# Attention, clustering and MLP on one core: the start of the first image, where two projections change their PSUM banks and one set of exponentials changes its place

## The chip, the cores and the metric

The kernel runs on one core of one Trainium2 chip. The metric is the device time of one execution in microseconds (us). The matmul engine is called PE here, the vector engine DVE, the scalar engine ACT, the GpSimd engine POOL, and SP is the engine that issues most of the transfers (DMAs).

## The reference, cut to what matters

Four images of 256 channels and 64 x 64 pixels (4096 positions) go through two layers. The change lies at the very start of the first layer, for the first image.

```python
def _L0_conv_ref(x, wq, bq, wk, bk, wv, bv, gamma):
    B, Cc, H, W = x.shape
    N = H * W                                   # 4096
    xf = x.reshape(B, Cc, N)
    q = jnp.einsum('oc,bcn->bno', wq, xf) + bq  # 32 channels
    k = jnp.einsum('oc,bcn->bon', wk, xf) + bk[None, :, None]
    attn = jax.nn.softmax(jnp.einsum('bnd,bdm->bnm', q, k), axis=-1)
    v = jnp.einsum('oc,bcn->bon', wv, xf) + bv[None, :, None]
    out = jnp.einsum('bcn,bmn->bcm', v, attn).reshape(B, Cc, H, W)
    return gamma[0] * out + x
```

The second layer (group norm, a 1x1 convolution into features and values, a clustering by the highest similarity, a projection, an MLP with a GELU, and two batch norms with ReLU) follows for each image. Only two of its details matter here: a small product of its weights, `wf`, is made at the start of the kernel, and its constants are worked out once on DVE (`derived`).

## The kernel before, in words

The order of all instructions is written out by hand (`tc.manual_schedule()`): each engine works through its own list in the order in which the program issues it, and waits by semaphores. Which buffer a tile gets is decided by the pools: a tile of a tag waits until the tile that had its buffer before has been read for the last time.

The attention of an image is cut into 64 units: 8 blocks of 512 queries by 8 groups of 512 keys. One unit `u` passes through these steps:

- `half(u, h)` for h = 0, 1 (line 420): PE makes two products of 128 keys by 512 queries into a tile `sc` of two PSUM banks; ACT copies it into `s` in SBUF (line 433); DVE takes the running maximum `top` (line 444).
- After the eight units of a block, the maximum is folded (line 501), turned over by PE (`turned_over`, line 506), reduced over keys and spread into a diagonal by DVE (`across`, lines 513 and 515), and broadcast by a matmul with ones into the tile `hold` (`spread`, line 573).
- `exps(u)`: DVE subtracts the maximum in two instructions (line 583), and ACT takes the exponentials in three (lines 588, 589, 592). The first writes into the second bank of `hold`.
- `factors(u)`: DVE forms `t31` (line 616, printed as tile `t`), and POOL forms further sums (line 595). They are the operands of a product by seven multiplications instead of eight.
- `weigh(u)`: PE multiplies them with the values into four banks `av` (line 679): first the term with `s` alone (`av<-s,v`), then the one with `t31` (`av<-t,v`).

For the first image the function `alone` brings the attention to the point where the loop over units begins. Its stages are: the values of the first half of the image; `staged("first")`, the projections of keys and queries of the first 2048 positions; more values; `staged("second")`, those of the other 2048 positions; then the eight units of block 0, with a pair of value tiles (`v_pair`) after each of the first six; then fold, turn-over, the first half of unit 8 (`half(GRP, 0)`, "the ninth score"), the last values, the broadcast, `wf`, the second half of unit 8, and `exps(0)` and `factors(0)`. After that `weighting` takes over: `exps(1)`, then `weigh(0)`, with the scores of later units between the parts.

A projection is stored "halved": ACT rounds it to a first half (line 335), DVE forms the rest (line 336), and SP writes four copies of these parts to DRAM for the keys and four for the queries (line 342). From there the units load their keys (`k_unit`, line 398) and queries (`q_block`, line 392). `staged` projects both keys and queries into one two-bank tile of the pool `ps_s` before it halves either; `halved` does it for one of them, in a one-bank tile of the pool `ps_m`, and its two parts go into a work buffer of the tag `t13`.

The pools in question have two buffers each:

```python
    ps_s = ctx.enter_context(tc.tile_pool(name="ps_s", bufs=2, space=PSUM))
    ps_m = ctx.enter_context(tc.tile_pool(name="ps_m", bufs=2, space=PSUM))
```

`ps_s` holds the scores `sc`, the tile of `staged`, and `hold` (which keeps one of its two buffers from the first broadcast on). `ps_m` holds the values `vp` (two halves to a tile, `v_half`, copied out by ACT at line 383), the turned-over maximum `tt`, the tile of `wf` (lines 256 and 259, copied out by ACT at lines 260 and 261), and two of the four banks `av`. `t31` lies in the tag `t13` too.

Of the kernel before, what the change touches and what calls it, by code (L numbers as in the profile page):

```python
# [29 lines left out]
RG, GRP = 4, N // NB  # L30
# [23 lines left out]
def attention_then_cluster_block(  # L54
# [197 lines left out]
    def wf():  # L252

        tps = ps_m.tile([P, NB], F32, tag="m", name="wf_p")
        for k in range(KC):
            nc.tensor.transpose(
                tps[:ED, k * P : (k + 1) * P], own_w["mix"][:, k, 0, 16 : 16 + ED], ident
            )
        nc.tensor.matmul(tps[:, C : C + ED], fb_w, ident[:ED, :ED], start=True, stop=True)
        nc.scalar.copy(wf_t, tps[:ED, :C])  # L260
        nc.scalar.copy(fvb[:, :ED], tps[:, C : C + ED])
# [43 lines left out]
    def attention(b, xs, ys):  # L305
# [7 lines left out]
        def projected(which, i, ps):  # L313

            col = 1 if which == "k" else 0
            for k in range(KC):
                for r in range(RG):
                    nc.tensor.matmul(
                        ps[r * D : (r + 1) * D],
                        wqk_s[:, k, col],  # L320
                        block(xs, k, 4 * i + r),
                        start=(k == 0),
                        stop=(k == KC - 1),
                    )

        def halves_of(which, i, hi, lo, ps, dma=nc.sync):

            col = 1 if which == "k" else 0
            if which not in own:
                own[which] = dram.tile([NBLK // RG, P, 4, NB], F32, tag=which, name=f"{which}_{b}")
            bias = bqk_s[:, col : col + 1]
            nc.scalar.activation(hi, ps, AF.Identity, bias=bias)
            nc.vector.scalar_tensor_tensor(
                lo, ps, bias, hi.bitcast(F32), ALU.add, ALU.subtract
            )
            rows = own[which][i]
            for c in range(4):  # L340
                part = hi if c in ((0, 2) if which == "k" else (0, 1)) else lo
                dma.dma_start(out=rows[:, c], in_=part.bitcast(F32))
# [6 lines left out]
        def staged(name, which, dma=nc.sync):  # L349


            st = spool.tile([P, 4, NB], F32R, tag="s", name=f"st_{b}_{name}")
            ps = ps_s.tile([P, 2, NB], F32, tag="s", name=f"pr_{b}_{name}")
            for j, (w, i) in enumerate(which):
                projected(w, i, ps[:, j])
            for j, (w, i) in enumerate(which):
                halves_of(w, i, st[:, 2 * j], st[:, 2 * j + 1], ps[:, j], dma)

        def halved(which, i):

            ps = ps_m.tile([P, NB], F32, tag="m", name=f"{which}p_{b}_{i}")
            two = work.tile([P, 2, NB], F32R, tag="t13", name=f"hl_{which}_{b}_{i}")
            projected(which, i, ps)
            halves_of(which, i, two[:, 0], two[:, 1], ps)
# [3 lines left out]
        def v_half(i):  # L368
            if i == 0:
                own["v"] = big.tile([P, N // P, C], F32, tag="v", name=f"v_{b}")  # L370
            if i % 2 == 0:
                vps[0] = ps_m.tile([P, 2, C], F32, tag="m", name=f"vp_{b}_{i // 2}")
            o = (i * P) % XT
            for k in range(KC):
                nc.tensor.matmul(  # L375
                    vps[0][:, i % 2, :],
                    xs[i * P // XT][:, k, o : o + P],
                    wv_s[:, k, :],
                    start=(k == 0),
                    stop=(k == KC - 1),  # L380
                )
            if i % 2:
                nc.scalar.copy(own["v"][:, i - 1 : i + 1, :], vps[0])

        def v_pair(i):
            v_half(2 * i)
            v_half(2 * i + 1)
# [12 lines left out]
        def begun(u):  # L400

            if u in slots:
                return
            nb, g = divmod(u, GRP)
            if u + 1 < units:
                k_unit(u + 1)

            pool, tag = {SLOTS: (swap, "w1"), SLOTS + 1: (swap, "w2")}.get(
                u % (SLOTS + 2), (spool, "s")
            )  # L410
            slots[u] = pool.tile([P, 4, 2, QW], F32, tag=tag, name=f"s_{b}_{u}")
            if g == 0:
                tops[nb] = work.tile([P, 2, NB], F32, tag="top", bufs=1, name=f"top_{b}_{nb}")
# [15 lines left out]
        def tiles(t):  # L429
            return t.rearrange("p r (h n) -> p r h n", h=2)  # L430

        def kept(u, h, sc):
            nc.scalar.copy(slots[u][:, PAIR[h]].rearrange("p h r n -> p r h n"), tiles(sc))  # L433
# [18 lines left out]
        def half(u, h, kept_only=False):  # L452

            nb, g = divmod(u, GRP)
            if h == 0:
                begun(u)
            sc = products(u, h)
            kept(u, h, sc)  # L460
            own_copy = slots[u][:, PAIR[h]].rearrange("p h r n -> p r h n")
            if g == 0 and h == 0:
                highest_of(nb, own_copy)
            elif g == 0 or kept_only:
                held.append(lambda: highest_of(nb, own_copy))
            else:
                return lambda: highest_of(nb, tiles(sc))
            return lambda: None
# [125 lines left out]
        def plus(out, x, y, op=ALU.add):  # L594
            nc.gpsimd.tensor_tensor(out, x, y, op)  # L595

        def factors(u):

            nb, g = divmod(u, GRP)
            s = slots[u]
            if g == 0:
                accs[nb] = work.tile([P, 2, 2, QW], F32, tag="acc", bufs=1, name=f"acc_{b}_{nb}")
            one, both = accs[nb][:, 0], accs[nb][:, 1]
            if g >= SEVEN:
                if g == SEVEN:
                    plus(both, both, one, ALU.subtract)
                for acc, q in ((both, B11), (one, B12), (both, B21), (one, B22)):
                    eng = nc.vector if acc is one and nb == NBLK - 1 else nc.gpsimd  # L610
                    eng.tensor_tensor(acc, acc, s[:, q], ALU.add)  # L611
                return
            b12 = own["hold"][:, 1].rearrange("p (r n) -> p r n", r=2).unsqueeze(1)
            t31[u] = work.tile([P, 2, 2, QW], F32, tag="t13", name=f"t13_{b}_{u}")
            t4s[u] = work.tile([P, 2, QW], F32, tag="t4", bufs=1, name=f"t4_{b}_{u}")
            nc.vector.tensor_tensor(  # L616
                t31[u], s[:, B11 : B22 + 1 : 2], b12.to_broadcast([P, 2, 2, QW]), ALU.add
            )
            plus(s[:, B12], t31[u][:, 1], s[:, B11])
            plus(t4s[u], s[:, B12], s[:, B21])  # L620
            if g == 0:
                plus(both, s[:, B12], s[:, B21])
            else:
                plus(one, t31[u - 1][:, 1] if g == 1 else one, t31[u][:, 1])
                plus(both, both, t4s[u])
# [183 lines left out]
        def alone():  # L809

            roots()
            for i in range(3):
                v_pair(i)
            staged("first", (("k", 0), ("q", 0)))
            k_unit(0)
            q_block(0)
            q_block(1)
            for i in range(3, 8):
                v_pair(i)
            for g in range(4):  # L820
                for f in sums(g):
                    f()
            for u in range(GRP):
                if u == 0:
                    begun(0)
                    staged("second", (("k", 1), ("q", 1)))
                    rest = load_rest()
                for h in range(2):
                    half(u, h)()
                caught(1)  # L830
                if u < 6:
                    v_pair(u + GRP)
                if u > 1:
                    next(rest, None)
            fold(0)
            for g in range(4, SEVEN):
                for f in sums(g):
                    f()
            tp = turned_over(0, ps_m.tile([P, 4, P], F32, tag="m", name=f"tt_{b}_0"))
            half(GRP, 0)  # L840
            v_pair(14)
            dgs["dg"] = across(0, "w2", tp)
            spread(0, dgs["dg"])
            v_pair(15)
            wf()
            half(GRP, 1)
            exps(0)
            factors(0)

        def maximum():  # L850
            dgs["dg"] = across(0, "t")
# [1187 lines left out]
```

## Time and profile before

| what | value |
|---|---|
| median of 3 runs | 3199.19 us (3198.45 to 3201.14) |
| the profiled execution, own time | 3196.98 us |
| its span, first to last instruction | 3195.0 us |
| PE busy | 3085.5 us, 97% of the span |
| DVE busy | 2537.0 us, 79% |
| POOL busy | 2260.6 us, 71% |
| ACT busy | 1734.8 us, 54% |
| mean granted PE clock | 0.990 |

Two microseconds of the profiled execution lie outside its span, and the execution is 2.2 us shorter than the median of the runs. Over the whole span PE is the engine with the least idle time; what a stage at the start is worth is read from its own waits, since all later work follows from it. The column PEclk of the tables by stretch is the share of full speed that the clock of PE was granted in that stretch; 0.50 means that matmuls ran at half speed.

### The profile page before, as it was taken

What the parts mean: (1) busy time and instruction counts of PE and PEld (TensorE: products, weight loads), DVE (VectorE), ACT (ScalarE), POOL (GpSimd) and SP (SyncE); (2) the same over time, 40 slices, a digit from 0 to 9 for tenths busy, and PEclk for the clock granted to TensorE, in tenths of its full rate; (3) what the DMA queues carried; (4) which work ended last, traced back from release to release, by engine and by line L of the source; (5) the groups of instructions that cost most, each with busy time, mean ns of one, the idle gap of its engine ahead of it and who ended that gap; (6) DMA issues with size and microseconds to landing.
All of it is one profiled execution on the core that took longest, in us unless ns stands there. A gap on an engine that the chain in (4) does not pass through costs nothing.

```text
span 3195.0 us, 40473 instructions
## 1 busy us (share of the span) xinstructions
PE 3085.5 (97%) x13890; PEld 2445.7 (77%) x13890; DVE 2537.0 (79%) x3649; ACT 1734.8 (54%) x2719; POOL 2260.6 (71%) x2127
## 2 busy tenths in 40 slices
PE   7999999999999999999999999999999999998999
PEld 5777887788677787768867788786876787875786
DVE  3888888677788888867778888877778888887675
ACT  4556654545556665445555666544556566654444
POOL 3888886378488888547848888855766888883663
PEclk8999999999999999999999999999999999999999
DMA  5122126100112123510011222431111112150000
GB/s 164 40 63 63 60 61 182 63 21 30 47 50 63 53 60 94 155 50 28 23 56 44 66 60 63 111 123 50 30 44 43 54 60 64 56 149 2 14 21 27
DMA packets 105868, 200.33 MB, mean 63 GB/s; under 512 B 14416, under 2 KB 30400, under 8 KB 104128
## 3 DMA queue, kind: packets, MB, share of 16 engines
q1 hardware_dynamic: 101856, 181.94, 17.9%
q0 software_dynamic: 2976, 14.70, 2.5%
q8 instruction: 110, 1.80, 0.2%
q10 hardware_dynamic: 832, 1.11, 0.1%
q14 instruction: 94, 0.77, 0.1%
HBM read 149.37 MB, written 48.34 MB: 62 GB/s over the span
## 4 chain that ended last, share of the span: by engine, by line
PE 42%; POOL 24%; DVE 19%; issue 8%; ACT 6%; DMA 1%; POOLq 0%; SPq 0%; ACTq 0%; DVEq 0%
PE mo L1651 10%; POOL acc L595 9%; PE av L679 6%; PE hq L1734 5%; DVE top L444 5%; DVE s L583 4%; POOL t L595 4%; POOL s L595 4%; DVE t L616 3%; PE hp L1734 3%; PE hr L1734 3%; PE fv L1225 3%; PE sc L420 3%; POOL acc L611 2%; PE vp L375 2%
## 5 line engine op out<-in xcount | busy, mean ns | idle before, releaser
L433 ACT COPY s<-sc 128x1024 f32<-128x1024 f32 x512 | 514.8, 1011 | 506.3 <-PE sc L420 500.1
L583 DVE TENSOR_TENSOR s<-s,hold 128x1024 f32<-128x1024 f32 x512 | 598.7, 1209 | 28.9 <-ACT hold L566 15.0
L595 POOL TENSOR_TENSOR s<-t,s 128x512 f32<-128x512 f32 x224 | 303.5, 1355 | 356.1 <-DVE t L616 287.6
L679 PE MATMUL av<-t,v 128*128 128x256 f32 x1792 | 464.8, 382 | 12.8 <-DVE t L616 11.7
L679 PE MATMUL av<-s,v 128*128 128x256 f32 x1792 | 460.8, 379 | 2.2 <-ACT s L589 2.2
L595 POOL TENSOR_TENSOR acc<-acc,t 128x512 f32<-128x512 f32 x352 | 461.2, 1329 | 0.0
L679 PE MATMUL av<-s,sum 128*128 128x256 f32 x1792 | 459.5, 379 | 0.0
L420 PE MATMUL sc<-q,k 128*128 128x512 f32 x1024 | 405.6, 480 | 36.8 <-DMA k<-k 10.5
L444 DVE TENSOR_TENSOR top<-sc,top 128x1024 f32<-128x1024 f32 x326 | 397.8, 1220 | 29.7 <-ACT s L433 24.8
L1689 ACT ACTIVATE hs<-hs,pv_s 128x256 f32<-128x256 f32 x496 | 232.3, 502 | 343.5 <-DVE hs L1725 343.5
L616 DVE TENSOR_TENSOR t<-s,hold 128x1024 f32<-128x1024 f32 x224 | 272.7, 1217 | 159.3 <-ACT s L592 71.0
L679 PEld LDWEIGHTS av<-t,v 128*128 128x128 f32 x1792 | 338.4, 190 | 70.1 <-DVE t L616 21.4
L1651 PE MATMUL mo<-hs,w 128*128 128x256 f32 x1512 | 385.3, 381 | 0.0
L679 PEld LDWEIGHTS av<-s,v 128*128 128x128 f32 x1792 | 340.3, 190 | 57.8 <-ACT s L589 2.6
L679 PEld LDWEIGHTS av<-s,sum 128*128 128x128 f32 x1792 | 339.4, 189 | 54.5 <-issue 1.9
L1651 PEld LDWEIGHTS mo<-hs,w 128*128 128x128 f32 x1512 | 283.0, 190 | 47.2 <-ACT hs L1689 6.4
L595 POOL TENSOR_TENSOR t<-s 128x512 f32<-128x512 f32 x224 | 295.7, 1320 | 17.6
L420 PEld LDWEIGHTS sc<-q,k 128*128 128x128 f32 x1024 | 176.6, 190 | 144.0 <-DVE top L444 70.2
L592 ACT ACTIVATE s<-s 128x1024 f32<-128x1024 f32 x256 | 267.5, 1045 | 1.2
L1725 DVE TENSOR_TENSOR hs<-hq,hs 128x256 f32<-128x256 f32 x496 | 198.8, 421 | 79.2 <-PE hq L1734 69.3
L588 ACT ACTIVATE hold<-s 128x512 f32<-128x512 f32 x224 | 135.1, 603 | 221.5 <-DVE s L583 221.4
L679 PE MATMUL av<-t,sum 128*128 128x256 f32 x896 | 231.7, 381 | 0.0
(299 smaller groups left out, 5349.1 us busy)
## 6 DMA issues: line engine op xcount, KB each, us to landing
k<-k SPq DMA_DIRECT2D x256, 256.0 KB, 2.7
x<-in_x SPq DMA_DIRECT2D x62, 512.0 KB, 6.6
out<-xn SPq DMA_DIRECT2D x62, 256.0 KB, 2.1
att<-t SPq DMA_DIRECT2D x56, 256.0 KB, 3.9
x<-att POOLq DMA_DIRECT2D x12, 1024.0 KB, 8.7
q<-q SPq DMA_DIRECT2D x32, 256.0 KB, 4.1
w<-in_w SPq DMA_DIRECT2D x8, 1024.0 KB, 10.3
rden<-row_rd SPq DMA_DIRECT2D x28, 256.0 KB, 3.7
```

Source lines behind the costliest of these rows:

```text
L420: nc.tensor.matmul(sc[:, r, :], k_s[:, (2 * h + r) * P : (2 * h + r + 1) * P], qs[u // GRP], start=True, stop=True,)
L433: nc.scalar.copy(slots[u][:, PAIR[h]].rearrange("p h r n -> p r h n"), tiles(sc))
L444: nc.vector.tensor_tensor(top, src, top if saved[nb] is None else saved[nb], ALU.max)
L583: nc.vector.tensor_tensor(sh, sh, mb.to_broadcast([P, 2, 2, QW]), ALU.subtract)
L592: nc.scalar.activation(s[:, PAIR[1]], s[:, PAIR[1]], AF.Exp)
L595: nc.gpsimd.tensor_tensor(out, x, y, op)
L616: nc.vector.tensor_tensor(t31[u], s[:, B11 : B22 + 1 : 2], b12.to_broadcast([P, 2, 2, QW]), ALU.add)
L679: nc.tensor.matmul(av[bank][:, half_ * QW : (half_ + 1) * QW], a[:, r], t[:, r], start=(g == 0 and r == 0 and i in (1, 7, 2, 4)), stop=(g ...
L1651: return nc.tensor.matmul(bank[:, half * HB : (half + 1) * HB], a[:, j], t, start=start, stop=stop)
L1689: nc.scalar.activation(src, src, AF.Gelu_apprx_tanh, bias=pvc("b1", P, j + 4 * (i > 1)))
L1725: nc.vector.tensor_tensor(dst, ps, term, ALU.add)
L1734: nc.tensor.matmul(out, w, x, start=True, stop=True)
```

## The change

In `alone`, the second projections go through `halved`, keys first, then queries, so they use two one-bank tiles of `ps_m` (the values' banks) in place of a two-bank tile of `ps_s`. After the turn-over, the pair of values 14 is split: one half is made ahead of the broadcast, the other after `exps(0)` and `factors(0)`. The pair 15, the second half of unit 8 and `wf` come after them too, and `wf` comes last.

```diff
             for u in range(GRP):
                 if u == 0:
                     begun(0)
-                    staged("second", (("k", 1), ("q", 1)))
+                    halved("k", 1)
+                    halved("q", 1)
                     rest = load_rest()
                 for h in range(2):
                     half(u, h)()
...
             tp = turned_over(0, ps_m.tile([P, 4, P], F32, tag="m", name=f"tt_{b}_0"))
             half(GRP, 0)
-            v_pair(14)
+            v_half(28)
             dgs["dg"] = across(0, "w2", tp)
             spread(0, dgs["dg"])
-            v_pair(15)
-            wf()
-            half(GRP, 1)
             exps(0)
             factors(0)
+            v_half(29)
+            v_pair(15)
+            half(GRP, 1)
+            wf()
```

`halved` is there before the change already, for the later images:

```python
        def halved(which, i):
            ps = ps_m.tile([P, NB], F32, tag="m", name=f"{which}p_{b}_{i}")
            two = work.tile([P, 2, NB], F32R, tag="t13", name=f"hl_{which}_{b}_{i}")
            projected(which, i, ps)
            halves_of(which, i, two[:, 0], two[:, 1], ps)
```

## The prediction

> **What bounds the kernel now.** I read the page first (PE busy 97% of the span), then the table by stretch of the first 160 us, then the chain of waits and the timelines of the two places that the diff touches. From 100 us on PE hardly waits (59.26 of 60 us busy); nothing after the start refers to absolute time, so what PE, DVE and ACT win together before 100 us should reach the end. The stretches (columns: stretch, length, busy us of PE, PE's weight loads, DVE, ACT, POOL, granted PE clock, DMA share, GB/s):
>
> ```profile
> 31.90:35.08 3.18, 0.70 (x2) 0.33 (x3) 1.50 (x2) 2.28 (x3) 0.00 (x0) 1.00 0.71 265
> 35.08:38.17 3.09, 3.09 (x10) 2.51 (x11) 1.23 (x1) 1.01 (x1) 0.00 (x0) 0.67 1.06 369
> ...
> 71.60:73.75 2.15, 0.00 (x1) 0.00 (x0) 0.00 (x0) 2.15 (x5) 0.00 (x0) 0.98 0.33 111
> 73.75:80.50 6.75, 6.53 (x15) 4.75 (x16) 5.82 (x5) 3.14 (x5) 4.44 (x3) 0.50 0.01 5
> ...
> 100.00:160.00 60.00, 59.26 (x253) 47.03 (x253) 53.65 (x51) 36.17 (x47) 49.43 (x38) 1.00 0.14 40
> ```
>
> PE stands twice, 2.4 us in the first line and 2.15 us in the third, and each time its clock drops afterwards (0.67 and 0.50). The first hole, in the chain of waits (start, us, what):
>
> ```profile
> 28.32 3.62 PE pr_second L318 x32
> ...
> 31.95 0.70 ACT st_second L335
> ...
> 32.68 0.76 DVE st_second L336
> ...
> 33.46 0.70 ACT st_second L335
> ...
> 34.19 0.76 DVE st_second L336
> ...
> 35.08 0.70 PE sc L420 x2
> 35.78 2.95 PE vp L375 x8
> 38.73 0.87 PE sc L420 x2
> ```
>
> The second score of unit 0 waits until DVE has halved both projections, because it takes the buffer of their tile. The second hole, in the timeline of ACT:
>
> ```profile
> 71.64 1.01 ACT L433 COPY s<-sc 128x1024 f32<-128x1024 f32 x1
> 72.55 0.61 ACT L588 ACTIVATE hold<-s 128x512 f32<-128x512 f32 x1
> 73.08 0.62 ACT L589 ACTIVATE s<-s 128x512 f32<-128x512 f32 x1
> 73.60 1.04 ACT L592 ACTIVATE s<-s 128x1024 f32<-128x1024 f32 x1
> 78.26 0.60 ACT L588 ACTIVATE hold<-s 128x512 f32<-128x512 f32 x1 [3.61 <-DVE s L583]
> ```
>
> and of PE:
>
> ```profile
> 70.53 0.38 PE L256 MATMUL wf_p<-ident,mix_first 128*96 128x128 f32 x2
> 70.75 0.36 PE L259 MATMUL wf_p<-ident,pv_s 96*128 96x96 f32 x2
> 70.89 0.71 PE L420 MATMUL sc<-q,k 128*128 128x512 f32 x2
> 73.75 2.08 PE L679 MATMUL av<-s,v 128*128 128x256 f32 x4 [2.15 <-ACT s L589]
> 76.05 2.05 PE L679 MATMUL av<-t,v 128*128 128x256 f32 x4 [0.21 <-DVE t L616]
> ```
>
> DVE has finished the subtractions at 71.36, but ACT copies values, `wf` and the score first; the first weighted product waits for the exponential of line 589.
>
> [...]
>
> **The change part by part.** *First edit.* No operation is added or removed: 32 projection matmuls, two instructions each on ACT and DVE (0.69, 0.75 us), eight writes and every load stay. Keys are done after 16 of the 32 matmuls, at 28.25 + 1.82 = 30.07, so ACT starts on them there and not at 31.95, and DVE ends at 31.6; queries run on ACT 31.95 to 32.64 (before: 33.46) and on DVE to 33.4 (34.95). The second tile's wait on ACT's copy of the values (28.94) is over in time. The two scores of unit 0 now use buffers free since 22.5: the first still starts at 32.0, when its queries land, the second at 32.7 (before 35.08). Values 8 need the keys' bank: free at 31.6, so they run 33.4 to 35.15, at full clock (1.74 us against 2.95 in the chain, 1.2 us). Scores of unit 1: 35.15 (38.73 in the chain); their two ACT copies end at 36.95 and 37.97, DVE's maxima at 38.2 and 39.45.
>
> SP's queue moves with it: four key writes from 30.83 (32.67), four query writes from 33.0 (34.87), so the load of keys 2, queued behind them, is issued at 35.35 (37.33). It took 3.4 us to land, with the DMA engines saturated; I take 3.4 to 3.7, so 38.75 to 39.05. That is late next: score 2 would be free at 38.2, so it starts at 39.0, not 41.95. The scores then fall into their old rhythm: its second half at 39.75 (43.28), DVE on it until 43.25 (46.32), **3.1 us** earlier. Bounds: 3.7 if keys 2 land by 38.2; 1.7 if the clock's 1.2 us is no gain (a window that misses the hole) and keys 2 land 0.2 us later. Keys 3 are issued by the end of score 1 (36.65) and land by 40; the weight loads behind them on SP move along. The new waits of `t31` on the eight writes (landed near 38) cost nothing.
>
> *Second edit*, in times of before, with the 3.1 us left out. Half of values 14 instead of all lies ahead of the broadcast: four matmul records of 0.215 us less, so `hold` ends at 68.1, not 68.97. DVE subtracts until 70.5 (71.36). ACT, now with nothing queued ahead, runs its three exponentials 70.57 to 72.66 (72.55 to 74.64), `t31` follows at 72.7 (74.68), and POOL's sums and `exps(1)` too: **DVE and POOL gain 2.0**. ACT then has queued behind the exponentials: values 14 to 73.2, values 15 to 73.7, score 8 to 74.6, `wf` to 75.1. All but one of these have late readers. The one is PE: `wf` takes the bank of values 14, so PE, through with score 8 at 71.2 (12 value records of 0.215 from 67.94, then 0.7), stands at `wf` until **73.2**, 2.0 us, about as long as before. Then `wf` (0.5 to 0.75) and the first weighted product at 73.7 to 73.95 (before: 73.75). Only the 0.21 us wait for `t31` falls away, and no score lies between.
>
> What this is worth depends on the clock. If the hole halves it again for two windows, products at 0.43 us each put score 9 at 77.4 and the product after it at 78.25 (78.74): PE gains **0.5**. If the clock stays full, PE would be 3.5 early by score 9's second half (79.3 against 82.88), but DVE and ACT, 2.0 early, then hold it (ACT's copy of score 10 ends at 88.5, PE wants it at 87.3): about 2.3. So the second edit gives 0.5 to 2.3; below, if DVE's delayed copies cost a wait that I don't see, -1. I take 0.5, because the hole is as long as the one that halved the clock before.
>
> Sum: 3.1 + 0.5 = 3.6 us. The profiled execution would go from 3196.98 to 3193.4 (span 3191.4). The median of the runs is 2.2 us above it, and the difference is carried over: 3199.19 - 3.6 = **3195.6**, 0.11% faster. A measurement of this kernel can tell about 0.2% (6.4 us) from no change.
>
> **The rivals.**
> 1. *Both edits pay in full:* keys 2 land early (3.7), and PE's hole misses the clock's windows with DVE no obstacle (3.5): 7.2 us, 3192.0; a little more if PE's later waits for DVE (1.5 us in the first 200) go too. For it: DVE and POOL gain 2.0 anyway. Against it: PE's queue at `wf`. Just faster than 0.2%.
> 2. *The first edit is hidden:* the eight writes and the loads share saturated DMA engines (share 1.06 at 35 to 38 us), keys 2 and 3 come hardly earlier, and the score loop starts where it did: 0 + 0.5, 3198.7. Against it: SP issues them 2 us earlier, and the engines were only 71% busy from 31.9 to 35.1.
> 3. *Slower, through the clock:* PE's new hole at `wf` or the shift by 3 us makes later weak stretches fall into clock windows. A stretch of two windows (6.8 us, as at 73.75) costs up to 3.4 us. Three more of them cost 10.2 and outweigh 3.6: 6.6 slower, 3205.8. It decides from two more on (6.8: slower at all), three for 0.2%. For it: the table shows half speed in further places (616, 1401, 2190, 2879, 2955 us), where PE is partly idle. Against it: [...]three runs before lie within 2.7 us.
> That the edits aren't in the program is excluded: the listing of instructions by engine shows both.
>
> **How the numbers follow.** The forecast (1.5 to 6.4 us faster) 0.55, rival 1 0.29, rival 2 0.08, rival 3 0.08. So faster 0.29, same 0.63, slower 0.08. The range: low end 3190.5, rival 1 with its extra 1.5; high end 3199.0, rival 2 with a spread of the runs; rival 3 is left out, and a tail of rival 1.
>
> **What would show it.** In the profile after: the second score of unit 0 right behind the first near 32.7, no clock of 0.5 at 36 us, keys 2 issued near 35.4, fold near 59.9 (62.98): the first edit. Three exponentials near 67.5 (72.55), `t31` near 69.6 (74.68), and PE idle for about 2 us ahead of `wf`, with the copy of values 14 as its releaser: the second. I am wrong if score 2 starts later than 41, if PE doesn't stand at `wf`, or if the gain at 100 us isn't there at the end.

## The result and the profile after

The changed kernel takes 3194.9 us (median of 22 runs, 3192.3 to 3197.4), the kernel before 3199.8 us beside it: a ratio of 0.9983, with a 95% interval from 0.9977 to 0.9989. That is about 5.4 us of gain, 0.17%. The prediction said 3195.6, 0.11% faster. The number was right. The sum behind it was not: of its two terms one paid nothing, the other paid more than I took, and by the account at the end more than half of the gain comes from something that the prediction doesn't contain.

First the profile after (span 3191.7 us, own time 3193.6 us). These are the stretches that answer to those shown before (stretch, length, busy us of PE, PE's weight loads, DVE, ACT, POOL, granted PE clock, DMA share, GB/s):

```profile
31.90:34.67 2.77, 2.77 (x17) 2.22 (x13) 0.82 (x2) 2.45 (x3) 0.00 (x0) 1.00 1.00 374
34.67:37.70 3.03, 3.00 (x14) 2.25 (x12) 2.34 (x2) 2.54 (x4) 0.00 (x0) 1.00 1.03 379
37.70:41.74 4.04, 0.00 (x0) 0.03 (x1) 1.34 (x2) 0.58 (x1) 0.00 (x0) 0.75 0.87 243
41.74:46.50 4.76, 4.76 (x11) 3.79 (x12) 2.38 (x2) 1.93 (x2) 0.00 (x0) 0.50 0.35 85
...
73.63:75.70 2.07, 0.00 (x1) 0.01 (x1) 0.49 (x1) 2.07 (x5) 0.00 (x0) 1.00 0.45 121
75.70:80.50 4.80, 4.80 (x24) 4.27 (x25) 4.80 (x5) 3.46 (x7) 3.92 (x3) 1.00 0.03 9
```

The first two lines show that the hole at the second score of unit 0 is gone: PE works without a stop at full clock from 31.9 to 37.7. The third shows what came in its place, a hole of 4.04 us with the DMA engines 87% busy, and the fourth what followed it, half speed (eight value products took 3.35 us there, from 43.59, and 1.89 us at full clock, from 47.70). The fifth is PE's stand at `wf`, and the sixth shows that the clock stayed at full speed after it. What PE waits for in the first 200 us (engine, line, what it waited for: us in total, times, longest):

```profile
PE sc L420 <- DMA k<-k: 5.7, 3, 4.1
...
PE wf_p L256 <- ACT v L383: 2.1, 1, 2.1
```

The longest of the first line's three waits, 4.1 us, is for the load of keys 2; the second line is for ACT's copy of the values. The queue of SP says why keys 2 are late (start, us, what):

```profile
31.21 2.16 SPq L342 DMA_DIRECT2D k<-hl_k  x4
33.48 3.14 SPq L342 DMA_DIRECT2D q<-hl_q  x4
36.71 1.28 SPq L398 DMA_DIRECT2D k<-k  x2
```

The eight writes take SP from 31.21 to 36.62, and keys 2, queued behind them, are issued at 36.71 and land at 41.61. The fold comes at 64.41; before it came at 62.98. Score 2 starts at 41.74, later than the 41 that the prediction named as a sign of being wrong. So at the fold the change is 1.4 us *behind* in this execution, at 100 us it is level, and it still ends 3.3 us ahead. The gain at the end is made later than 100 us, where the prediction had none.

### The profile page after: what moved, and what is told of

Same layout as the page of the kernel before. It is cut to its first block, busy times and chain, and to the rows that moved or that the text cites. A ratio compares the mean times of both kernels' runs of the same rounds, so it can differ in the third digit from the quotient of the medians.

```text
span 3191.7 us, 40464 instructions
## 1 busy us (share of the span) xinstructions
PE 3081.7 (97%) x13890; PEld 2449.4 (77%) x13890; DVE 2535.0 (79%) x3649; ACT 1734.1 (54%) x2719; POOL 2260.7 (71%) x2127
## 4 chain that ended last, share of the span: by engine, by line
PE 44%; POOL 22%; DVE 18%; issue 7%; ACT 6%; DMA 2%; SPq 0%; POOLq 0%; ACTq 0%; DVEq 0%
PE mo L1653 10%; POOL acc L595 8%; PE av L679 8%; PE hq L1736 5%; DVE s L583 4%; DVE top L444 4%; POOL t L595 4%; POOL s L595 4%; DVE t L616 4%; PE hp L1736 3%; PE hr L1736 3%; PE fv L1227 3%; PE sc L420 3%; POOL acc L611 2%; PE vp L375 2%
```

## Experiments 1 and 2: each edit alone

The first edit alone (in the kernel before):

```diff
-                    staged("second", (("k", 1), ("q", 1)))
+                    halved("k", 1)
+                    halved("q", 1)
```

> The first edit alone: second keys and queries halved by way of the values' banks, everything after the turn-over as before. Theory A (the eight writes and the load of keys 2 share saturated DMA engines, so keys 2 land near 41 us and score 2 can't start earlier than before): within 1.5 us of before, fold near 63 to 65 us. Rival B (the profiled execution of the changed kernel had a late landing by chance; usually score 2 starts near 39 us): about 3 us faster than before, fold near 60 us, and most of the 4.9 us of the whole change are here.

Measured: 3196.6 us, ratio 0.9987 (0.9979 to 0.9996), so about 4.2 us of gain. The second edit alone is the changed kernel with `staged("second", ...)` put back.

> The second edit alone: the exponentials of unit 0 ahead of the second half of values 14, values 15, score 8's second half and the product of weights; the second projections as before. Theory A: most of the 4.9 us are here, 3 to 5 us faster than before, since PE's clock stays up more often and DVE and POOL run 1 to 2 us ahead. Rival B: 0.5 to 2 us faster. In the profile of both: the three exponentials near 70.5 us, PE idle for 2 us ahead of the product of weights, its first weighted product near 73.7 us.

Measured: 3197.5 us, ratio 0.9993 (0.9985 to 1.0002), about 2.2 us. The two add up to 6.4 us, roughly the whole. The second is near its rival B. But the profile of the first edit alone has its fold 30.55 us after unit 0's first score; the kernel before needed 30.98. There is hardly anything there to make 4 us of: on the first edit alone theory A was right about the fold, rival B about the time, and neither about both.

## Experiments 3 and 4: remove the two waits

The late keys: the second queries' four writes are issued after unit 2, so that the loads of keys 2 and 3 go ahead of them (cut: `halves_of` and `halved` also get the argument `later`, a list that keeps the writes back).

```diff
-                    halved("q", 1)
+                    later = []
+                    halved("q", 1, later)
...
+                if u == 2:
+                    later.pop()()
```

> The changed kernel, with the four writes of the second queries to DRAM issued after the loads of keys 2 and 3 and of the mixing weights instead of ahead of them (nothing reads them before block 4). Theory A: keys 2 are issued near 33.5 us and land near 37.5, score 2 starts near 38.5 us instead of 41.7, and the kernel is about 3 us faster than the changed one, 7 to 8 us faster than before. Rival B: keys 2 don't set the start in most executions; no more than 1 us faster than the changed kernel.

The wait at `wf`: its tile moves out of the values' banks.

```diff
-        tps = ps_m.tile([P, NB], F32, tag="m", name="wf_p")
+        tps = ps_a.tile([P, NB], F32, tag="a1", name="wf_p")
```

> The changed kernel, with the tile of the product of weights in a bank of the weighted products (ps_a, not yet in use) instead of the values' bank, so PE doesn't wait there for ACT's copy of values 14. Theory A: the idle 2 us of PE ahead of it go, the first weighted product starts when its exponential is done, about 1.5 us earlier, but the product after it waits for t31 of DVE; 0.5 to 1.5 us faster than the changed kernel, more where the clock would have dropped in that hole. Rival (PE is not what sets the pace there, DVE is): no difference, within 0.5 us.

Both did what they should in the profile. The lines of the late writes (seven further down in the code), of SP and of PE:

```profile
33.74 2.87 SPq L405 DMA_DIRECT2D k<-k  x2
...
38.18 0.73 PE L427 MATMUL sc<-q,k 128*128 128x512 f32 x2 [0.20 <-DVE top L451]
```

Keys 2 are issued at 33.74 and not 36.71, score 2 starts at 38.18 and not 41.74, and the fold comes 5.4 us earlier, at 59.00. With `wf` elsewhere PE doesn't stand there at all. The times: 3194.9 us (0.9983, 0.9977 to 0.9990) for the late writes, the same as the changed kernel; 3194.5 us (0.9979, 0.9973 to 0.9986) for `wf`, which leaves open whether moving it is worth the 0.5 to 1.5 us expected. So the late keys are shown to be what delays the fold, and yet 5 us won at the fold gave nothing at the end that these runs can tell (some 2 us to either side). A lead over the changed kernel of 4.8 us at 128 us was 3.0 us at 300 us and gone at 1600 us. Two questions were open: where the first edit's time comes from, and where this lead goes.

## Experiments 5 to 8: the ring of score tiles

The first edit does one thing besides changing banks. `staged` takes a tile from `spool`, the ring that the score tiles come from; `halved` takes its halves from `work`. So every later tile of the ring stands one buffer earlier. This can be had alone: the kernel before, with the joint two-bank projection kept, but the halves put into the two `work` tiles.

```diff
-                    staged("second", (("k", 1), ("q", 1)))
+                    ps = ps_s.tile([P, 2, NB], F32, tag="s", name=f"pr_{b}_second")
+                    for j, w in enumerate("kq"):
+                        projected(w, 1, ps[:, j])
+                    for j, w in enumerate("kq"):
+                        two = work.tile([P, 2, NB], F32R, tag="t13", name=f"hl_{w}_{b}_1")
+                        halves_of(w, 1, two[:, 0], two[:, 1], ps[:, j])
```

> The kernel before with one thing of the first edit alone: the halves of the second keys and queries stand in the two work tiles that the edit uses, so the ring of score tiles in SBUF is no longer moved on by one; the projections stay together in the two banks of a score, so PE's wait of 2.4 us at unit 0's second score stays. Theory (the first edit's gain of about 4 us in the timed runs is worked at the start, by the bank): no difference from before, ratio 0.9995 to 1.0005. Rival (it comes from the ring of score tiles, which sets later waits of ACT's copies): most of the 4 us is here, ratio 0.9987 to 0.9990.

Measured: 3196.5 us, ratio 0.9989 (0.9982 to 0.9995). The rival has it: this alone is worth about 3.5 us, while PE still stands 2.5 us at the second score and the fold comes 31.12 us after unit 0's first score. By the ratios (an interval of 1.6 to 5.8 us) the first edit's gain is nearly all here, and in the profile none of it is at the start.

On the same chip as this experiment ran second profiles of both kernels and the two remedies of experiments 3 and 4 together.

> The kernel before, unchanged, for a second profile of it. If the time from the start of unit 0's first score to the fold is a property of the kernel, it is again 31.0 us (30.98 in the first profile), the wait of the second score on DVE is 2.4 us, and the span is some 2 to 5 us above the first profile's, which was faster than every timed run of this kernel. If the start varies from execution to execution by more than the 1.4 us that separate the kernels there, one profile of each cannot say what the first edit is worth, and the timed runs must.

Measured: one time, 3198.8 us, and the fold 30.53 us after unit 0's first score (30.98 in the first profile): in the kernel before that distance repeats within half a microsecond, and the moment of unit 0's score is not (33.82 here, 32.00 there).

> The changed kernel, unchanged, on the same chip as the next two, for its ratio and a second profile. Theory (the gain is worked before the fold and in the last score, and stays): ratio 0.9983, about 5 us under before. In the profile keys 2 are issued 4.0 to 4.7 us after unit 0's second score starts and land 4 to 5 us later, PE stands about 4 us for them, and again 2.07 us at wf. Rival (keys 2 came late by chance in the first profile): they land within 3.7 us of their issue, score 2 starts 6.5 to 7 us after unit 0's first score (9.7 in the first profile), and the fold is 28 us after it (32.3).

Measured: 3194.4 us, ratio 0.9985 (0.9977 to 0.9992). Keys 2 are issued 4.50 us after unit 0's first score (3.92 after its second, a little less than expected) and land 4.44 us later; PE stands 3.5 us for them and 2.05 at `wf`; the fold is at 32.23. The late keys are no chance event.

> The changed kernel with two things more: the second queries' four writes are issued after unit 2, behind the loads of keys 2 and 3, and wf stands in another bank than values 14. Theory A (early time is kept to the end): keys 2 land 5 us earlier and the fold with them, PE does not stand at wf, first weighted product 6.5 us earlier than in the changed kernel: 6 us under it, ratio to before 0.996. Theory B (what is won ahead of 100 us is given back in the first two blocks, as the profile of the late writes alone showed: a lead of 4.8 us at 128 us, 3.0 at 300 us): the time is that of the changed kernel within 1.5 us, ratio 0.9978 to 0.9985, and the profile shows the lead shrinking between 128 and 300 us again.

Measured: 3191.8 us, ratio 0.9973 (0.9963 to 0.9984). Theory A asked for 6 us under the changed kernel, theory B for none. Beside the changed kernel on the same chip (3194.4) it is 2.6 us. It is the first kernel that clearly beats the changed one.

## Where the ring's time is: every 128th record

I laid the traces side by side, instruction by instruction, and looked for places after 130 us at which all kernels with the ring moved differ from all those without. They are few and sharp. Here are two of them, in the timelines of DVE (start, us, what). Before, the end of block (3,0)'s row, and the fold of a later block:

```profile
2113.55 1.53 DVE L724 SCALAR_TENSOR_TENSOR t<-av,pv_s,t 128x512 f32<-128x512 f32 x3 [0.46 <-DVE t L712]
...
2511.18 1.74 DVE L501 TENSOR_TENSOR top<-top 128x512 f32<-128x512 f32 x1
```

and the same instructions after:

```profile
2112.73 1.53 DVE L724 SCALAR_TENSOR_TENSOR t<-av,pv_s,t 128x512 f32<-128x512 f32 x3
...
2508.12 0.69 DVE L501 TENSOR_TENSOR top<-top 128x512 f32<-128x512 f32 x1
```

In the first place DVE stood 0.46 us before, 0.10 us after. (Its line says it waited for DVE's own result, but that result is equally early in both.) In the second the same fold takes 1.74 us or 0.69.

The key is *which* instruction stands. I counted ACT's records in the trace from the start (instructions, and the semaphore records that an instruction with several waits brings along). Before, ACT stands 0.32 us more than its waits explain at its 320th, 1344th, 1472nd, 1984th and 2240th records. After, it does so at the 1344th, 2240th, 2752nd, 3008th and 3264th. Each is a multiple of 128 plus 64. DVE's stop at 2113 us is its 2880th record, again 22 x 128 + 64. In profiles with the same length of stream the stops come at the same records (of these, the 320th shows in one profile only, and a 3392nd in some). In all 14 profiles no other instruction of ACT or DVE after 100 us starts more than 0.2 us later than its waits explain. I read this as a short stop at every 128th record of a stream, which shows only where the engine has no slack. (POOL has many other delays; among them are stops of 0.32 to 0.37 us at its 1221st, 2885th and 3013th records in the changed kernel, each 69 above a multiple of 128. Why its count is five off I can't say.)

The traces also hold a DMA queue that the profile calls `q14 instruction`. In the span of either kernel it moves 94 packets of 8192 bytes (0.77 MB on both pages), and the streams of ACT, DVE, POOL and SP together have 95 places 64 above a multiple of 128. Over the 14 profiles 71 stops of ACT show after 50 us; in 68 of them such a packet starts 0.64 to 0.97 us after the delayed instruction (before: the stop at 1221.00, the packet at 1221.65). So the stops and these packets go together in time. What holds the engine is not shown; no run changes these packets by themselves.

The ring moves these stops. With the other order of the ring some instructions have fewer semaphores to wait for, so fewer records: ACT has 3510 and not 3515, DVE 4494 and not 4496, POOL 3016 and not 3018, and all nine that are missing are semaphore records. Five records on, ACT's stop falls on another instruction for the rest of the program.

A stop of 0.3 us becomes a whole microsecond in the following way. ACT's copies of scores around the fold, before (in brackets: idle time and what ended it):

```profile
2505.01 1.01 ACT L433 COPY s<-sc 128x1024 f32<-128x1024 f32 x1 [0.88 <-PE sc L420]
2508.88 1.01 ACT L433 COPY s<-sc 128x1024 f32<-128x1024 f32 x1 [0.86 <-PE sc L420]
```

and after:

```profile
2502.24 1.01 ACT L433 COPY s<-sc 128x1024 f32<-128x1024 f32 x1 [1.17 <-PE sc L420]
2505.82 1.01 ACT L433 COPY s<-sc 128x1024 f32<-128x1024 f32 x1 [0.57 <-PE sc L420]
```

After, the stop of 0.3 us is at the earlier copy (the 2752nd record), the next copy stands 0.57 us and not 0.86, and DVE comes to its fold 0.3 us sooner relative to POOL. (That the one leads to the other is inferred from these lines; the padded kernels below test it.) POOL at that moment, before and after:

```profile
2511.10 1.28 POOL L595 TENSOR_TENSOR t<-s 128x512 f32<-128x512 f32 x1
```

```profile
2508.34 1.61 POOL L595 TENSOR_TENSOR t<-s 128x512 f32<-128x512 f32 x1
```

Before, POOL's instruction starts 0.08 us ahead of DVE's fold (2511.10 and 2511.18) and the fold takes 1.74 us. After, DVE starts 0.22 us ahead (2508.12 and 2508.34), takes 0.69, and it is POOL that is stretched. The other profiles agree on the fold: in the five with 3515 records of ACT POOL starts 0.07 to 0.08 us ahead and the fold takes 1.74 to 1.76 us, in the nine with 3510 DVE starts first and the fold takes 0.7. The one that starts second pays 1.05 us on DVE (1.74 against 0.69) and 0.33 on POOL (1.61 against 1.28); the other's instruction still had 1.20 and 0.47 us to go. What makes it wait, the traces don't show.

## Experiments 9 to 12: put the stops back

If the place in the stream is what counts, then a few instructions that do nothing, run at the start where the engines are idle, must undo the gain. All nine, in the changed kernel:

```diff
+    pads = const.tile([P, 3, 8], F32, name="pads")
+    for j in range(5):
+        nc.scalar.activation(pads[:, 0, j : j + 1], probe, AF.Sqrt)
+    for j in range(2):
+        nc.vector.memset(pads[:, 1, j : j + 1], 0.0)
+    for j in range(2):
+        nc.gpsimd.memset(pads[:, 2, j : j + 1], 0.0)
```

> The changed kernel plus nine instructions of one column each, run in the first 12 us where their engines stand idle: five on ACT, two on DVE, two on POOL. They do no needed work; they put each engine's stream of instructions back to the length that it has in the kernel before (3515, 4496 and 3018 records in the trace; the changed kernel has 3510, 4494 and 3016), so that every later instruction has the place in its stream that it had before. Theory (an engine stands 0.3 to 0.4 us at every 128th record of its stream, and most of the first edit's gain in the timed runs is that these stops fall elsewhere): the ring's gain of about 3 us goes, time 3197 to 3199, ratio 0.9992 to 0.9997; in the profile DVE's subtraction at the end of block (3,0)'s row, L724, waits 0.46 us again (0.10 in the changed kernel), PE's hole there is 1.5 us, not 1.2, the fold near 2508 us takes 1.74 us again, not 0.69. Rival (the gain is in waits that the ring's other order takes away): the nine cost nothing, time and ratio as for the changed kernel, 0.9983 to 0.9985.

Measured: 3197.9 us, ratio 0.9994 (0.9986 to 1.0002). The places are as before again:

```profile
2116.73 1.53 DVE L731 SCALAR_TENSOR_TENSOR t<-av,pv_s,t 128x512 f32<-128x512 f32 x3 [0.46 <-DVE t L719]
...
2513.71 1.76 DVE L508 TENSOR_TENSOR top<-top 128x512 f32<-128x512 f32 x1
```

(The lines of the code are seven further down.) Next the five on ACT alone, then the two on DVE with the two on POOL.

> The changed kernel plus only the five small instructions on ACT. Theory (place in the stream): only the places that hang on ACT's stops come back: the fold near 2508 us at 1.74 us and the 0.24 us near 1221 us, about 1 to 2 us in all, time 3196 to 3197, ratio 0.9987 to 0.9991; DVE's L724 in block (3,0) still waits 0.10 us. Rival: as the changed kernel, 0.9983 to 0.9985.

> The changed kernel plus only the two small instructions on DVE and the two on POOL. Theory (place in the stream): DVE's L724 in block (3,0) waits 0.46 us again and PE's hole there is 1.5 us, with a half-speed window of 3.4 us behind it in some executions (1.5 us), and DVE's square near 1372 us takes 1.47 us again, not 0.55: 1.3 to 2.8 us in all, time 3196 to 3198, ratio 0.9987 to 0.9992; the fold near 2508 us stays at 0.69 us. Rival: as the changed kernel, 0.9983 to 0.9985.

Measured: 3197.3 us, 0.9993 (0.9985 to 1.0002), and 3197.4 us, 0.9994 (0.9986 to 1.0002). The places follow the engine whose stream was padded. ACT's five, DVE's two places:

```profile
2115.06 1.53 DVE L727 SCALAR_TENSOR_TENSOR t<-av,pv_s,t 128x512 f32<-128x512 f32 x3
...
2510.94 1.75 DVE L504 TENSOR_TENSOR top<-top 128x512 f32<-128x512 f32 x1
```

DVE's and POOL's four:

```profile
2114.32 1.53 DVE L728 SCALAR_TENSOR_TENSOR t<-av,pv_s,t 128x512 f32<-128x512 f32 x3 [0.46 <-DVE t L716]
...
2510.99 0.69 DVE L505 TENSOR_TENSOR top<-top 128x512 f32<-128x512 f32 x1
```

In one it is the fold that is slow, in the other the stop at L724 is back. In time each half costs nearly as much as all nine, somewhat more than its places explain, and both ratios lie just above the range expected; the two halves don't add up, and with intervals of some 2.7 us to either side I leave that open. That the padding delays the start instead is not so: unit 0's first score comes at 32.1 to 33.8 us in these three profiles, at 32.0 to 34.0 in the others. The changed kernel wasn't timed beside them. Its ratios from elsewhere, 0.9983 and 0.9985, are what the 0.9993 and 0.9994 of the three padded kernels are set against; each ratio is to the kernel before on the same chip.

The last run pads POOL by one record in the fastest kernel, which had 3015.

> The kernel with the late writes and wf in another bank, which was at 0.9973, plus one small instruction on POOL, which makes POOL's stream 3016 records long, as in the changed kernel, instead of 3015. Theory (place in the stream): DVE's square near 1372 us takes 0.55 us, not 1.47, as in the changed kernel and unlike the kernel without the pad; 0.8 us won, time near 3191, ratio 0.9970 to 0.9973. Rival: the square stays at 1.47 us, time 3191.8.

Measured: 3191.0 us, ratio 0.9974 (0.9964 to 0.9984). The square near 1367 us takes 0.55 us, as the theory has it, where the kernel without the pad needs 1.46:

```profile
1370.20 1.46 DVE L1217 TENSOR_TENSOR vf<-vf 128x384 f32<-128x384 f32 x1
```

```profile
1367.48 0.55 DVE L1220 TENSOR_TENSOR vf<-vf 128x384 f32<-128x384 f32 x1
```

The timed runs can't tell the two kernels apart: they ran on different chips, and the ratios are 0.9973 without the pad and 0.9974 with it. But the traces bear on the open question of the late writes: the code of that experiment had made DVE's stream 4495 and POOL's 3015 records long. Against the changed kernel it lost 0.5 us near 290 us, 0.35 near 1302, 0.8 at the square, 0.5 near 1400, 0.6 near 1555 and 0.25 near 1895, the same in both kernels with those lengths. These 3 us are what was left of the lead at 300 us. The losses at the square, near 1400 and near 1555, some 1.8 us, are not there in the kernel with the pad, which keeps 4.5 of its 5.5 us of lead at 128 us to the end of its profile. That is more than the timed runs show, and stays open. The part that was lost before 300 us has another cause: PE stood 2.4 us at a score at 190.88 us, and in the run with DVE and POOL padded it stood 2.5 us near there for a load of keys.

## Why the prediction was right, and where it wasn't

**The second score of unit 0: right.** It starts at 32.66, as predicted (32.7), and unit 1 at 34.67 (35.15).

**Keys 2: the step that failed.** This is the term of 3.1 us. I had them issued at 35.35 and landed by 39.05, with SP's issues as long as before. SP's query writes came right behind the key writes, with the DMA engines at a share of 1.03 to 1.05 from 33.48 to 36.62; four of them took 3.14 us to issue, and the load 4.90 us to land against the 3.4 to 3.7 that I took. Score 2 started at 41.74, not 39.0. The late writes show that this queue is the cause: with the load ahead of the query writes score 2 starts at 38.18. The term of 3.1 us at the fold measured nothing, or a loss of 0.7: over seven profiles with the first edit and its queue the fold is 31.5 us after unit 0's first score on average (29.9 to 32.6), over four with the old start 30.8 (30.5 to 31.1). Score 2 did come 0.8 us sooner on average (9.1 us after unit 0's first score, not 9.9), but the new hole mostly brings half speed behind it: with no half-speed window there the fold was at 29.9 (one profile), with one at 30.6 (two), with two at 32.2 to 32.6 (four). Rival 2, the first edit hidden by saturated DMA engines, was right here.

**The second edit: right in mechanism, small in size.** PE stands 2.07 us at `wf` for ACT's copy of the values, where I had 2.0. I took the lower bound, 0.5, because I let the clock halve after it. In this profile it didn't (clock 1.00 in the line 75.70:80.50); over all profiles with that hole a half-speed window followed in four of seven. From the fold to a fixed product near 130 us the second edit gains 1.6 us on average (70.6 without, 69.0 with), inside the stated 0.5 to 2.3; without the hole (`wf` in another bank) it would be 2.6.

**The clock: the number had no single answer.** In all 14 profiles the half-speed stretches start on a grid of 3.413 us, called windows here as in the prediction, whose phase to the kernel's start differs from execution to execution: the first such stretch that is recorded starts at 36.12 us in the profile before and at 39.70 after, 1.99 and 2.15 us past a multiple of 3.413. In these two profiles each of them lasts one, two or three windows (3.41, 6.83 or 10.24 us), but for the last, which runs to the end of the record. What the fall goes with, in these traces, is how busy PE was in the window before. The changed kernel, cut along its own grid:

```profile
32.87:36.29 3.42, 3.42 (x17) 2.92 (x16) 1.98 (x2) 3.15 (x5) 0.00 (x0) 1.00 1.03 382
36.29:39.70 3.41, 1.38 (x7) 0.88 (x5) 2.45 (x2) 1.77 (x3) 0.00 (x0) 1.00 0.97 280
39.70:43.11 3.41, 1.37 (x3) 1.16 (x4) 0.00 (x0) 0.14 (x1) 0.00 (x0) 0.50 0.55 190
43.11:46.53 3.42, 3.42 (x9) 2.65 (x8) 2.41 (x2) 1.79 (x2) 0.00 (x0) 0.50 0.42 95
46.53:49.94 3.41, 3.22 (x15) 2.44 (x14) 1.38 (x3) 2.73 (x4) 0.00 (x0) 1.00 0.34 95
```

A window with PE 40% busy (1.38 of 3.41) is followed by one at 0.50, one that is full by one at 1.00. Over the 14 profiles, from 12 to 16 us on, where the record of the clock begins, windows at full clock with PE busy under 42% were followed by half speed in 120 of 120 cases, windows above 54% never, and in between it went either way. So a hole of 2 us costs a window in some executions and not in others; the prediction priced it as certain, and one profile of each kernel cannot show a difference of 2 us. Nor does every such window cost something at the end: one at 490 us took 1.4 us from the changed kernel's profile against that of the late writes, and by 521 us 1.2 us of it was made up.

**What wasn't in the sum: the stops.** The places that I could name after 130 us are 0.24 us near 1221, 0.82 at the square, 0.37 at 2113, about 0.9 around the fold at 2511, less 0.17 near 3083: 2.2 us. At 2113 PE's hole is 1.5 us with the stop and 1.2 without. With the stop a window is only 52% busy, on the edge, and in three of five such profiles a half-speed window follows that costs 1.5 us; without it, in none of nine. That adds 0.9 us on average (an estimate, 3 of 5 times 1.5): some 3.1 us, against 3.0 (medians) to 3.5 (ratio) measured with the ring alone. In the traces, three profiles with the old ring lose 2.9 us between 200 us and the end to five with the new one, on average.

So the sum that the profiles support is: first edit at the start about -0.7, second edit 1.6, stops 3.1, together 4.0; measured 4.9 (medians) to 5.4 (ratio), an interval of 3.5 to 7.4. The prediction's 3.6 was 3.1 + 0.5. That it came so close is luck in its parts.

**The rivals.** Rival 1 asked for keys 2 by 38.2 and no clock loss: not so. Rival 3 had the idea that a shift at the start changes something thousands of instructions later. It does, but not through the shift in time: through the count of records, and here to the good.

## What to carry to other kernels

When two versions differ by a few tenths of a percent, compare the traces instruction by instruction over the *whole* span before believing that the gain is where the edit is; then pad the streams back to their old lengths to see what the edit itself is worth. A load that the critical path waits for belongs ahead of writes in its queue: here, with the DMA engines at a share of 1.0, moving four writes behind two loads brought the fold from 31.5 to 26.9 us after unit 0's first score, on average (in the timed runs this alone gained nothing that shows). Price a hole in PE by the chance that half speed follows it (here, after a hole of 2 us, in four of seven profiles), not by one profile.

The fastest versions here, 3191.8 and 3191.0 us (0.9973 and 0.9974), have the change, the late query writes and `wf` in another bank.

## What the runs showed of the hardware that I had not expected

- Stops at records 64 above a multiple of 128 in an engine's stream, 0.32 us on ACT (before, its 1344th record, at 1221.00) and 0.4 us on DVE (before, its 2880th, at 2113.55), visible where the engine has no slack. In 68 of 71 on ACT a packet of 8192 bytes on the queue `q14 instruction` starts 0.64 to 0.97 us after the delayed instruction.
- A DVE instruction took 0.69 us or 1.74 (the fold), and 0.55 or 1.46 (the square), the short time where it started ahead of POOL's and the long time where it started behind. A lead of 0.08 us of POOL was enough for the one, a lead of 0.09 of DVE for the other (the square at 1367.48, POOL at 1367.57).
- SP's issue of a DMA took 0.32 us for the first two key writes (the DMA engines at a share of 0.80 and 1.01), 0.45 and 0.51 us for the other two (0.93 and 0.99), and 0.57 to 1.08 us for the query writes right behind them (1.04 over 33.48 to 36.62).
